# Output stage of two scan layers: scaling moved from GpSimd to ScalarE, and the code of a position arranged as a pipeline

## The chip, the cores and the metric

The kernel runs on one core of one Trainium2 chip. The metric is the device time of one execution in microseconds (us). Times of several executions are given as a median with the lowest and the highest. The profile is that of one further execution, and its span is the time from its first to its last instruction. Engine names are those of the profile: PE is TensorE, PEld its weight loads, DVE is VectorE, ACT is ScalarE, POOL is GpSimd, and SP is the engine that issues most DMAs.

## The reference

The input `x` has 4 batches of 64 x 64 positions with 192 channels, in float32. Two layers follow each other, and each adds its result to its input:

```python
x = x + _L0_conv_ref(_gn(x), ...)
x = x + _L1_conv_ref(_gn(x), ...)
```

Both layers have the same frame. The input is normalised by groups and projected to 768 channels, of which 384 are the values and 384 the gate `z`. The values go through four selective scans (by rows, by columns, and both backwards; layer 1 of the reference has a small convolution in front), and the four results are summed to `y`, with 384 channels at each of 4096 positions. What the change touches is what comes after that sum, here as the second layer has it:

```python
y = y1 + y2 + y3 + y4
mu = jnp.mean(y, axis=-1, keepdims=True)
var = jnp.mean(jnp.square(y - mu), axis=-1, keepdims=True)
y = (y - mu) * jax.lax.rsqrt(var + 1e-05) * gamma + beta
y = y.reshape(B, H, W, D_INNER) * jax.nn.silu(z)
return y @ W_out
```

So each position is normalised over its own 384 channels, scaled and shifted by channel, multiplied by the gate, and projected back to 192 channels.

## The kernel before

Layer 1 below is the reference's layer 0, layer 2 its layer 1. `FirstLayer.run` is called once for each of the 4 batches: it projects, scans (most of the time), and calls `finish` with a list of this one batch. `SecondLayer.run` is called once for all batches: it projects, prepares and scans the four, then calls the same `finish` with a list of four. So `finish` runs five times in an execution: four times with one batch, once with four. In the profile the tiles of layer 1 carry `_f` at the end of weight names, those of layer 2 `_s`; results of layer 1 go to `mid`, those of layer 2 to `out`.

`finish` works on tiles of 512 positions (`LC`), 8 of them in a batch (`NCH`), called positions 0 to 7 in this text. One tile holds `yt`, the summed `y` with positions on the 128 partitions (4 blocks, `NJ`, of 384 channels), and `zg`, the gate with channels on the partitions (3 blocks, `ND`, of 512 positions). Its steps are:

- `start` (L865) is called once for a batch. It issues the loads of `yt` and `zg` of all 8 positions (L870, L873) and the Silu of each `zg` on ScalarE (L874). Then, in two groups, positions 0 and 1 and positions 2 to 7, it takes mean and variance of every position on VectorE (L882, L883, into `mv`), the square root on ScalarE (L885) and the reciprocal on VectorE (L886, `rs`), and lets GpSimd subtract the mean and multiply by `rs`, in place, one block of 128 positions with 384 channels in an instruction (L891): four instructions for a position.
- The loop at L897 then goes through the positions: TensorE turns the 12 squares of 128 x 128 into `vp` with channels on the partitions (L905), ScalarE copies each of the three `vp` to `v` with scale gamma and bias beta (L908), VectorE multiplies `v` by the gate (L911), TensorE multiplies by `w_out` into four `op` (L916), VectorE adds the layer's input `xl` to each (L919), and SP stores the result (L920).
- For layer 2, `start` of the next batch stands in the code after position 4 of the current one (L921).

The order of the instructions on each engine in `finish` isn't written by hand. The scans are enclosed in a manual schedule, but `finish` is not: a scheduler orders what is there by the code order, the data dependences and the free buffers of the pools. Each engine then takes its instructions strictly in that order, SP its DMAs too. The pools that matter are `fy` and `fz` with 10 buffers each (so `yt` and `zg` of 8 positions and of 2 more), `fw` with 3 (`v`, `ot`, `st`), `fl` with 3 (`xl`), `fm` with 4 PSUM banks (`vp`) and `fo` with 4 (`op`).

In the built program before, TensorE's order in layer 1 is: transposes of positions 0 and 1, products of 0 and 1, transposes of 2 to 4, products of 2 to 4, transposes of 5 to 7, products of 5 to 7.

Of the kernel before, what the change touches and what calls it, by code (L numbers as in the profile page):

```python
# [10 lines left out]
F32 = mybir.dt.float32  # L11
AF = mybir.ActivationFunctionType
ALU = mybir.AluOpType

NB, HW, CH = 4, 64, 192
L = HW * HW
DI, NS, DR, KD = 384, 16, 12, 4
ND = DI // 128
CB, NC2 = 96, 2
LC = 512  # L20
NCH = L // LC
# [3 lines left out]
NJ = LC // 128  # L25
# [377 lines left out]
class FirstLayer:  # L403
# [449 lines left out]
    def finish(self, batches):  # L853

        nc, tc = self.tc.nc, self.tc
        with ExitStack() as ctx:
            pool = lambda name, bufs, **k: ctx.enter_context(tc.tile_pool(name=name, bufs=bufs, **k))
            py, pz, pl, ps, pw = pool("fy", 10), pool("fz", 10), pool("fl", 3), pool("fs", 2), pool("fw", 3)
            pm = pool("fm", 4, space=bass.MemoryType.PSUM)
            po = pool("fo", 4, space=bass.MemoryType.PSUM)  # L860
            w_out = ctx.enter_context(tc.tile_pool(name="fc", bufs=1)).tile([128, ND, CH], F32, name="w_out")
            nc.sync.dma_start(w_out, self.w["w_out"])
            pos = lambda a, t: a[t * LC : (t + 1) * LC, :].rearrange("(j p) c -> p j c", p=128)

            def start(y, gate):  # L865

                yts, zgs = [], []
                for t in range(NCH):
                    yt = py.tile([128, NJ, DI], F32, name="yt")
                    nc.sync.dma_start(yt, pos(y, t))  # L870
                    yts.append(yt)
                    zg = pz.tile([128, ND, LC], F32, name="zg")
                    nc.sync.dma_start(zg, gate[t])  # L873
                    nc.scalar.activation(zg, zg, AF.Silu)  # L874
                    zgs.append(zg)
                for lo, hi in ((0, 2), (2, NCH)):
                    n = (hi - lo) * NJ
                    mv = ps.tile([128, n, 2], F32, name=f"mv{lo}")
                    for t in range(lo, hi):
                        st = pw.tile([128, NJ, nc.vector.BN_STATS_DIM], F32, name="st")  # L880
                        for j in range(NJ):
                            nc.vector.bn_stats(st[:, j, :], yts[t][:, j, :])  # L882
                            nc.vector.bn_aggr(mv[:, (t - lo) * NJ + j, :], st[:, j, :])  # L883
                    rs = ps.tile([128, n], F32, name=f"rs{lo}")
                    nc.scalar.activation(rs, mv[:, :, 1], AF.Sqrt, bias=self.ln_eps)  # L885
                    nc.vector.reciprocal(rs, rs)  # L886
                    for t in range(lo, hi):
                        for j in range(NJ):
                            i = (t - lo) * NJ + j
                            part = yts[t][:, j, :]  # L890
                            nc.gpsimd.tensor_scalar(part, part, mv[:, i, 0:1], rs[:, i : i + 1], ALU.subtract, ALU.mult)  # L891
                return yts, zgs

            ready = start(batches[0][2], batches[0][3])
            for b, (src, dst, _, _) in enumerate(batches):
                yts, zgs = ready
                for t in range(NCH):  # L897
                    yt, zg = yts[t], zgs[t]
                    xl = pl.tile([128, NJ, CH], F32, name="xl")
                    nc.sync.dma_start(xl, pos(src, t))  # L900
                    v = pw.tile([128, ND, LC], F32, name="v")
                    for d in range(ND):
                        vp = pm.tile([128, LC], F32, name="vp")
                        for j in range(NJ):
                            nc.tensor.transpose(  # L905
                                vp[:, j * 128 : (j + 1) * 128], yt[:, j, d * 128 : (d + 1) * 128], self.ident
                            )
                        nc.scalar.activation(  # L908
                            v[:, d, :], vp, AF.Identity, bias=self.beta[:, d : d + 1], scale=self.gamma[:, d : d + 1]
                        )  # L910
                    nc.vector.tensor_mul(v, v, zg)  # L911
                    ot = pw.tile([128, NJ, CH], F32, name="ot")
                    for j in range(NJ):
                        op = po.tile([128, CH], F32, name="op")
                        for d in range(ND):
                            nc.tensor.matmul(  # L916
                                op, v[:, d, j * 128 : (j + 1) * 128], w_out[:, d, :], start=(d == 0), stop=(d == ND - 1)
                            )
                        nc.vector.tensor_add(ot[:, j, :], op, xl[:, j, :])  # L919
                    nc.sync.dma_start(pos(dst, t), ot)  # L920
                    if t == NCH // 2 and b + 1 < len(batches):  # L921
                        ready = start(batches[b + 1][2], batches[b + 1][3])


class Chunk:
# [651 lines left out]
```

## Time and profile before

| what | before |
|---|---|
| median of 3 runs | 11391.58 us (11390.1 to 11404.04) |
| span of the profiled execution | 11398.9 us |
| busy: PE, DVE, ACT, POOL | 84%, 85%, 85%, 79% of the span |
| mean granted TensorE clock | 0.926 of full speed |
| one output stage of layer 1, first `yt` load to last add | 2401.3 to 2501.8 us, the other three alike |
| output stage of layer 2 | 11095.2 to 11392.4 us |

A group of the profile names the line, the engine, the operation with its output and inputs, the shapes and the count; then come its total busy time, the mean of one, and the idle time of its engine just before it with what ended that idle time. A float32 matmul leaves two records, so the 768 products of L916 stand there as 1536. The view by windows gives the busy time of every engine in a stretch, the clock that TensorE was granted (1.00 is full speed), the share in which the 16 DMA engines were busy, and what they moved. The chain of waits follows the end back to what released it. An average over the whole execution says little here, since the scans take over four fifths of it and load all engines evenly; the output stages have to be read by themselves.

### The profile page before, as it was taken

The numbers are of one execution on the slowest core, as the hardware profiler recorded it, in microseconds if no ns is written. First come the engines' busy times: TensorE is split into PE (matmuls) and PEld (weight loads), VectorE is DVE, ScalarE is ACT, GpSimd is POOL, SyncE is SP. The second block draws the span as 40 slices with busy tenths as digits, with TensorE's granted clock in tenths as the row PEclk, the third lists the DMA queues.
The fourth block names the chain that finished last, engine by engine and source line by source line (L and its number), as shares of the span: only waits on it lengthen the run. The fifth ranks groups of instructions, "written<-read, shape, count | busy, mean of one in ns | idle before, by whom it ended". The sixth has DMA issues, their size and how long they took to land. (4 is left out here: it accounts for less than half of the span.)

```text
span 11398.9 us, 171795 instructions
## 1 busy us (share of the span) xinstructions
PE 9629.2 (84%) x61449; PEld 7328.0 (64%) x61449; DVE 9660.8 (85%) x11508; ACT 9638.7 (85%) x16730; POOL 9049.1 (79%) x3032
## 2 busy tenths in 40 slices
PE   7998888878998888878988888779988888788667
PEld 4776666655776666646766666647766666555356
DVE  4999899966999899948999899849998999788455
ACT  5999999957999999939999999849999999665554
POOL 3999899956999899938999899839998999700468
PEclk8999999988999999988999999979999999889678
DMA  4333334444333334443333334433333443433446
GB/s 125 108 105 97 94 99 98 100 127 122 108 103 100 93 99 99 97 156 97 109 102 96 96 97 103 123 119 108 108 99 94 98 103 98 128 120 127 144 117 238
DMA packets 831027, 1269.85 MB, mean 111 GB/s; under 512 B 99002, under 2 KB 514631, under 8 KB 829652
## 3 DMA queue, kind: packets, MB, share of 16 engines
q1 hardware_dynamic: 825300, 1252.49, 39.3%
q0 software_dynamic: 4864, 6.29, 0.4%
q8 instruction: 488, 8.00, 0.3%
q14 instruction: 375, 3.07, 0.1%
HBM read 958.19 MB, written 300.42 MB: 110 GB/s over the span
## 5 line engine op out<-in xcount | busy, mean ns | idle before, releaser
L738 POOL TENSOR_TENSOR h<-h,bct 128x1536 f32<-128x1536 f32 x2048 | 7062.7, 3470 | 577.6 <-DVE carry L734 475.8
L724 DVE TENSOR_TENSOR_SCAN h<-a,carry,x 128x512 f32<-128x512 f32 x5376 | 6605.9, 1267 | 226.8 <-PE x L716 184.5
L716 PE MATMUL x<-ident,xT 128*128 128x128 f32 x24576 | 4000.0, 287 | 815.7 <-DVE h L724 713.6
L699 ACT ACTIVATE xT<-dtuT,bT 128x384 f32<-128x384 f32 x8192 | 4360.0, 610 | 91.6 <-PE x L716 87.0
L716 PEld LDWEIGHTS x<-ident,xT 128*128 128x128 f32 x24576 | 2803.7, 145 | 2139.0 <-DVE h L724 926.3
L711 ACT ACTIVATE a<-dt,A_log_f 128x512 f32<-128x512 f32 x6144 | 3978.8, 717 | 0.0
L751 PE MATMUL yp<-ident,h 128*128 128x128 f32 x24576 | 3703.4, 277 | 9.3 <-POOL h L738 9.1
L751 PEld LDWEIGHTS yp<-ident,h 128*128 128x128 f32 x24576 | 2945.6, 144 | 78.8 <-issue 63.1
L615 PE MATMUL dp<-xd,w_dtb_f 13*128 13x512 f32 x1536 | 890.1, 663 | 208.0 <-DVE dt L644 206.9
L724 DVE TENSOR_TENSOR_SCAN h<-a,x 128x512 f32<-128x512 f32 x768 | 899.0, 1207 | 191.2 <-PE x L716 113.4
L628 POOL TENSOR_SCALAR wl<-e 128x1536 f32<-128x1536 f32 x128 | 189.3, 1479 | 699.0 <-ACT e L624 381.0
L891 POOL TENSOR_SCALAR yt<-yt,mv,rs 128x384 f32<-128x384 f32 x256 | 466.9, 1837 | 200.1 <-DVE rs L886 187.0
L490 PE MATMUL pp<-xT,w_in 96*128 96x512 f32 x1152 | 536.9, 617 | 0.0
L615 PEld LDWEIGHTS dp<-xd,w_dtb_f 13*128 13x128 f32 x1536 | 238.7, 192 | 452.1 <-DVE dt L644 336.1
L745 PE MATMUL yp<-yold,ident 128*128 128x512 f32 x768 | 440.8, 659 | 72.6 <-DMA yold<-y 72.6
L621 ACT ACTIVATE e<-dp 128x512 f32<-128x512 f32 x384 | 224.8, 585 | 307.8 <-DVE dt L644 153.5
L1094 DVE SCALAR_TENSOR_TENSOR acc<-pad,conv_w_s,acc 128x2048 f32<-128x2048 f32 x192 | 439.2, 2343 | 52.6 <-ACT acc L1092 51.9
L641 POOL TENSOR_TENSOR e<-e,wl 128x1536 f32<-128x1536 f32 x128 | 444.9, 3476 | 0.3
L638 POOL TENSOR_TENSOR e<-e,dt 128x1536 f32<-128x1536 f32 x128 | 442.8, 3459 | 0.3
L905 PE MATMUL vp<-ident,yt 128*128 128x128 f32 x768 | 163.6, 361 | 305.4 <-POOL yt L891 303.6
L1075 POOL MEMSET pad<- 128x66 f32 x12 | 1.9, 159 | 508.1 <-DVE acc L1094 489.3
L490 PEld LDWEIGHTS pp<-xT,w_in 96*128 96x128 f32 x1152 | 222.4, 198 | 253.4 <-issue 244.6
(171 smaller groups left out, 7173.9 us busy)
## 6 DMA issues: line engine op xcount, KB each, us to landing
bct<-xp SPq DMA_DIRECT2D x1024, 512.0 KB, 4.9
uT<-uT SPq DMA_DIRECT2D x64, 768.0 KB, 4.7
yold<-y SPq DMA_DIRECT2D x64, 768.0 KB, 8.0
y<-yt SPq DMA_DIRECT2D x64, 768.0 KB, 4.3
uT<-uT SPq DMA_DIRECT2D x128, 384.0 KB, 5.3
yold<-y SPq DMA_DIRECT2D x128, 384.0 KB, 5.3
y<-yt SPq DMA_DIRECT2D x128, 384.0 KB, 4.6
yt<-y SPq DMA_DIRECT2D x64, 768.0 KB, 10.4
```

Source lines behind the costliest of these rows:

```text
L490: self.tc.nc.tensor.matmul(pp, self.w_in[:, i, e * 128 : (e + 1) * 128], self.xT[:, i, t * LC : (t + 1) * LC], start=(i == 0), stop=(i == ...
L615: nc.tensor.matmul(self.dp[d], w, self.xd[0 : DR + 1, :], start=True, stop=True)
L638: nc.gpsimd.tensor_tensor(self.e, self.e, self.dt, ALU.subtract)
L641: nc.gpsimd.tensor_tensor(self.e, self.e, self.wl, ALU.add)
L699: nc.scalar.mul(xTs[g][:, j, :], it.dtuT[:, j * DI : (j + 1) * DI], it.bT[:, j, n : n + 1])
L711: nc.scalar.activation(as_[g][:, d, :], it.dt[:, d, :], AF.Exp, scale=scale)
L716: nc.tensor.transpose(xs[g, d][:, j * 128 : (j + 1) * 128], xTs[g][:, j, d * 128 : (d + 1) * 128], ident)
L724: nc.vector.tensor_tensor_scan(along(hs[g][:, d, :], it.k), along(as_[g][:, d, :], it.k), along(xs.pop((g, d)), it.k), 0.0 if it.first els ...
L738: nc.gpsimd.tensor_tensor(hs[g], hs[g], bc(cs[g - n % 2][:, n % 2, :], 1, ND), ALU.mult)
L745: nc.tensor.matmul(it.yp[b], ident, yo, start=True, stop=False, skip_group_check=True)
L751: nc.tensor.matmul(it.yp[b][:, i * 128 : (i + 1) * 128], hs[g][:, d, j * 128 : (j + 1) * 128], ident, start=False, stop=n == NS - 1, is_tr ...
L891: nc.gpsimd.tensor_scalar(part, part, mv[:, i, 0:1], rs[:, i : i + 1], ALU.subtract, ALU.mult)
```

## The change

`start` no longer scales the positions. It computes one more small vector per group, `off`, which is minus the mean times `rs`, on VectorE, and hands out `rs` and `off` for each position. A new function `gated` does, for one position, the scaling in place on ScalarE (`yt * rs + off`, four instructions), then the transposes, the copies to `v` and the product with the gate. A new function `out` does the load of `xl`, the products with `w_out`, the adds and the store. The loop runs over all positions of all batches in one list: `gated` of position t + 1 stands ahead of `out` of position t, also from one batch to the next, and `start` of the next batch stands at position 4 as before, though now ahead of that position's `out`. Nothing is left for GpSimd in `finish`. The pools keep their sizes.

```diff
             def start(y, gate):
-                yts, zgs = [], []
+                r = []
                 for t in range(NCH):
...
                     rs = ps.tile([128, n], F32, name=f"rs{lo}")
                     nc.scalar.activation(rs, mv[:, :, 1], AF.Sqrt, bias=self.ln_eps)
                     nc.vector.reciprocal(rs, rs)
+                    off = ps.tile([128, n], F32, name=f"off{lo}")
+                    nc.vector.scalar_tensor_tensor(off, mv[:, :, 0], -1.0, rs, ALU.mult, ALU.mult)
                     for t in range(lo, hi):
-                        for j in range(NJ):
-                            i = (t - lo) * NJ + j
-                            part = yts[t][:, j, :]
-                            nc.gpsimd.tensor_scalar(part, part, mv[:, i, 0:1], rs[:, i : i + 1], ALU.subtract, ALU.mult)
-                return yts, zgs
+                        part = slice((t - lo) * NJ, (t - lo + 1) * NJ)
+                        r[t] += [rs[:, part], off[:, part]]
+                return r
+
+            def gated(yt, zg, rs, off):
+                for j in range(NJ):
+                    part = yt[:, j, :]
+                    nc.scalar.activation(part, part, AF.Identity, scale=rs[:, j : j + 1], bias=off[:, j : j + 1])
+                v = pw.tile([128, ND, LC], F32, name="v")
+                for d in range(ND):
+                    vp = pm.tile([128, LC], F32, name="vp")
+                    for j in range(NJ):
+                        nc.tensor.transpose(
+                            vp[:, j * 128 : (j + 1) * 128], yt[:, j, d * 128 : (d + 1) * 128], self.ident
+                        )
+                    nc.scalar.activation(
+                        v[:, d, :], vp, AF.Identity, bias=self.beta[:, d : d + 1], scale=self.gamma[:, d : d + 1]
+                    )
+                nc.vector.tensor_mul(v, v, zg)
+                return v
+
+            def out(src, dst, t, v):
+                xl = pl.tile([128, NJ, CH], F32, name="xl")
+                nc.sync.dma_start(xl, pos(src, t))
+                ot = pw.tile([128, NJ, CH], F32, name="ot")
+                for j in range(NJ):
+                    op = po.tile([128, CH], F32, name="op")
...
+                    nc.vector.tensor_add(ot[:, j, :], op, xl[:, j, :])
+                nc.sync.dma_start(pos(dst, t), ot)
-            ready = start(batches[0][2], batches[0][3])
-            for b, (src, dst, _, _) in enumerate(batches):
-                yts, zgs = ready
-                for t in range(NCH):
...
-                    if t == NCH // 2 and b + 1 < len(batches):
-                        ready = start(batches[b + 1][2], batches[b + 1][3])
+            flat = [(b, t) for b in range(len(batches)) for t in range(NCH)]
+            ready = {0: start(*batches[0][2:])}
+            v = gated(*ready[0][0])
+            for i, (b, t) in enumerate(flat):
+                if t == NCH // 2 and b + 1 < len(batches):
+                    ready[b + 1] = start(*batches[b + 1][2:])
+                more = None
+                if i + 1 < len(flat):
+                    b1, t1 = flat[i + 1]
+                    more = gated(*ready[b1][t1])
+                out(batches[b][0], batches[b][1], t, v)
+                v = more
```

In the built program after, TensorE's order in layer 1 is: transposes of positions 0 and 1, products of 0 and 1, transposes of 2 and 3, products of 2, then transposes of t + 1 and products of t in turn up to 7. In layer 2 it is the same within a batch; from one batch to the next, the products of the last three positions stand behind the first transposes of the new batch.

More of the change, by code (lines that the diff above doesn't have):

```diff
@@ L870, in start @@
                     nc.sync.dma_start(yt, pos(y, t))
-                    yts.append(yt)
                     zg = pz.tile([128, ND, LC], F32, name="zg")
@@ L874, in start @@
                     nc.scalar.activation(zg, zg, AF.Silu)
-                    zgs.append(zg)
+                    r.append([yt, zg])
                 for lo, hi in ((0, 2), (2, NCH)):
@@ L881, in start @@
                         for j in range(NJ):
-                            nc.vector.bn_stats(st[:, j, :], yts[t][:, j, :])
+                            nc.vector.bn_stats(st[:, j, :], r[t][0][:, j, :])
                             nc.vector.bn_aggr(mv[:, (t - lo) * NJ + j, :], st[:, j, :])
@@ L892, in start @@
-                return yts, zgs
-            ready = start(batches[0][2], batches[0][3])
-            for b, (src, dst, _, _) in enumerate(batches):
-                yts, zgs = ready
-                for t in range(NCH):
[L898 to L901, printed above, removed]
-                    for d in range(ND):
[L903 to L909, printed above, removed]
-                        )
[L911 to L920, printed above, removed]
-                    if t == NCH // 2 and b + 1 < len(batches):
-                        ready = start(batches[b + 1][2], batches[b + 1][3])
@@ new lines, in out @@
+            def out(src, dst, t, v):
[4 more added lines that the diff above has]
+                    op = po.tile([128, CH], F32, name="op")
+                    for d in range(ND):
+                        nc.tensor.matmul(
+                            op, v[:, d, j * 128 : (j + 1) * 128], w_out[:, d, :], start=(d == 0), stop=(d == ND - 1)
+                        )
+                    nc.vector.tensor_add(ot[:, j, :], op, xl[:, j, :])
+                nc.sync.dma_start(pos(dst, t), ot)
```

## The prediction

> **What bounds the kernel now.** I read the page's groups first, because the diff touches one function, the output stage `finish`: which instruction there is long, and who waits for it.
>
> ```profile
> L891 POOL TENSOR_SCALAR yt<-yt,mv,rs 128x384 f32<-128x384 f32 x256 | 466.9, 1837 | 200.1 <-DVE rs L886 187.0
> L905 PE MATMUL vp<-ident,yt 128*128 128x128 f32 x768 | 163.6, 361 | 305.4 <-POOL yt L891 303.6
> ```
>
> GpSimd scales the positions (466.9 us), and TensorE stood idle 303.6 us for it. The scans' work cannot hide that, since each output stage runs after its scans. Next the busy time of each engine by stage: layer 2's output stage, then one output stage of layer 1 in tens of microseconds.
>
> ```profile
> 11095.00:11392.50 297.50, 208.15 (x1153) 191.14 (x1153) 167.75 (x425) 137.57 (x153) 238.27 (x128) 0.80 0.73 249
> 2401.30:2501.90 100.60, 56.39 (x289) 50.06 (x289) 43.47 (x106) 36.12 (x39) 56.76 (x32) 0.69 0.55 190
> ...
> 2421.00:2431.00 10.00, 5.77 (x22) 4.75 (x22) 2.57 (x3) 5.97 (x8) 6.19 (x4) 0.50 1.04 395
> 2451.00:2461.00 10.00, 5.28 (x21) 3.86 (x20) 1.76 (x1) 4.02 (x6) 10.00 (x6) 0.50 0.00 0
> 2471.00:2481.00 10.00, 10.00 (x64) 9.98 (x64) 5.49 (x12) 0.00 (x0) 10.00 (x7) 1.00 0.53 154
> ```
>
> Columns: PE, PEld, DVE, ACT and POOL busy, granted TensorE clock, DMA share, GB/s. In layer 2's stage GpSimd is busy 80%, TensorE 70%, and ScalarE, at 46%, is the emptiest. From 2451 GpSimd alone is full and TensorE runs at half clock; the loads (395 GB/s) are over by then. Then the timeline at the end of that stage:
>
> ```profile
> 2444.17 42.86 POOL L891 TENSOR_SCALAR yt<-yt,mv,rs 128x384 f32<-128x384 f32 x24 [16.98 <-DVE rs L886]
> ...
> 2480.74 3.26 PE L905 MATMUL vp<-ident,yt 128*128 128x128 f32 x26
> 2481.38 4.12 ACT L908 ACTIVATE v<-vp,beta_f,gamma_f 128x512 f32<-128x512 f32 x6 [11.86 <-PE vp L905]
> ...
> 2489.06 12.37 PE L916 MATMUL op<-w_out,v 128*128 128x192 f32 x72
> ...
> 2501.88 1.08 PE L454 MATMUL tp<-ident,xl 128*96 128x128 f32 x8 [0.45 <-DVE ot L919]
> ```
>
> The 24 pieces of positions 2 to 7 run at 1.79 us each; TensorE takes transposes of three positions and then the output products of three, so 12.37 us of products stand bare after the last piece; the next batch starts 0.05 us after the last add (2501.83). The other three batches repeat it (windows of 101, 101 and 102 us). For layer 2 the chain of waits shows the same pair:
>
> ```profile
> 11235.50 28.76 POOL yt L891 x15
> 11264.27 0.04 issue
> 11264.31 2.18 PE vp L905 x9
> 11266.49 16.97 PE op L916 x96
> ```
>
> **What the Trainium skill says.** (1) "ScalarE: Activation LUTs", section What ACT_TABLE_LOAD costs: an activation takes 186 ns, 93 more for each per-partition operand, 0.833 ns an element, and neighbours overlap by 93. The trace agrees: 512 columns with scale and bias as operands (L908) would be 798 and took 777; 384 with one (L699) would be 599 and took 610. (2) Same page, Table sets: identity is in every set, so a scaling between Silu and Sqrt needs no load. The trace agrees: at 11285.02 nine L908 run right behind the Sqrt at L885. (3) "TensorE: Matmul & The Clock Gate", Part 1: half clock until about 3.4 us of sustained work. The rows above show 0.50 beside gaps and 1.00 when full. (4) "GPSIMD Engine Reference", Engine selection: one-input work at roughly line rate. Here the measurement differs and decides: 384 columns with two per-partition operands took 1643 ns, 1536 with immediates (L628) 1477.
>
> **The change part by part.**
>
> Removed: 256 GpSimd pieces, 128 in each layer. Added: 256 ScalarE activations. From L908 less 128 columns (L711 717 less L699 610, so 107 ns) one is 670 ns alone; L908 in threes takes 2.11 us, a pitch of 0.667, so 0.56 in a row, 2.24 a position. Bounds 0.50 (L699's pitch) to 0.67. Further 16 small vector products `off` of 8 or 24 columns, priced as the reciprocals beside them (0.20 and 0.30 us); one per group lies on the path: 0.3 us a batch. No table load is added: the built program has as many as before. DMAs are the same in number. The program outside `finish` keeps its order but for one weight load and a handful of setup products between the layers, cost nothing: the long setup around them hides them.
>
> ScalarE then has per position Silu 1.40 (4 in 5.59), scaling 2.24 and three v 2.1: 5.7 us, where GpSimd had 4 x 1.64 = 6.6 alone and 4 x 1.86 = 7.4 in layer 2 (59.68 us for 32). The new activation waits for `off` from VectorE; behind it on ScalarE stand the v of the position before and the next Silu, and TensorE waits for both. VectorE per position: statistics 2.55, product 1.76, four adds 1.4, 5.7 us. TensorE at full clock: 12 transposes 1.5 (26 records in 3.26) and products 3.9 (an add every 0.975): 5.4 us; at half clock 2.6 (9 in 2.18) and 7.8. DMA: 2 x 768 KB and 2 x 384 KB, 2.36 MB, at the 393 GB/s of the full windows, 6.0 us. So GpSimd's 7.2 is followed by four engines within a tenth of each other. That is why I do not take the whole of the removed 467 us.
>
> Moved: in the built order TensorE has transposes of t+1 ahead of products of t for positions 2 to 6, one by one in place of by threes. The load of `xl` and the store of a position now follow the next position's work in the code; in the built SP queue three `xl` loads still stand ahead of the first `yt`, and the next batch's loads behind two stores, as before: nothing. GpSimd's queue has nothing left in the stage that could wait.
>
> *Layer 1, one batch.* On VectorE the statistics of positions 4 and 5 now stand ahead of the product of position 1. That product ends near 2431.1 (v ready at 2429.3, by laying ScalarE's order out with the times above; it was 2432.04). After it come 3 adds, statistics 6, 5 adds, statistics 7, some 7.7 us, then Sqrt 0.3, reciprocal 0.3, `off` 0.3: 2439.7 instead of 2444.1. ScalarE loads its table and does a last Silu (2.8): 2442.5. Six scalings (3.3), three v (2.1), the product (1.8): first output product at 2449.7. From there TensorE is the longest: 6 products x 3.9 and 4 transposes x 1.5, 29.4 us, and 1.7 for 3.4 us at half clock: 2480.8, with the last add 2481.2. ScalarE has 24 x 0.56 + 18 x 0.70 = 26 us from 2442.5, done at 2468.6 beside it; VectorE 19. Gain 2501.8 - 2481.2 = 20.6 us, for four batches 82. Ends: TensorE warm at once and ScalarE the limit, 27; TensorE cold for half of it, 12.
>
> *Layer 2.* The same start, 8693.9 us later by the first loads (2401.30 and 11095.21), gives `off` of the first batch at 11134 (GpSimd started 11139.06). ScalarE's work from there: 30 positions x 5.74, less 5 Silu done, plus 13 table loads x 1.28 and six Sqrt: 184 us. TensorE has 30 x 5.4 = 162, VectorE about 158, DMA 61.7 MB / 393 = 157. Between the batches the order is worse: products of positions 5 to 7 stand behind the first transposes of the next batch, and VectorE's adds behind its statistics. Laying the order out once, I get TensorE idle about 7 us and then 12 us of products in a row at each of three boundaries. I take a tenth of ScalarE's 184 as lost, 203, and 5 us for the last product and add: 11342 against 11392.4. Gain 51. Ends: no loss and no new waits, 68; a quarter lost, 25.
>
> Sum: 82 + 51 = 133 us. Against the profiled span of 11398.9 that is 11266. The profiled execution lies 7.3 us above the median of the three runs (11390.1 to 11404.04), so I forecast 11391.6 - 133 = 11258 us.
>
> **The rivals.**
>
> A. ScalarE is the only limit; TensorE stays warm. For: 10.00 of 10.00 busy at clock 1.00 from 2471. Against: 5.4 of 5.7 leaves nothing for gaps. 4 x 27 + 65 = 173 us: 11219.
>
> B. The loads become layer 2's limit. For: DMA shares of 1.02 to 1.05 in four of the stage's sixteen 20 us windows already, and 10 buffers, so the next batch's loads wait for a position to be used up and stand behind stores in SP's queue. Against: 75.5 MB need 192 us of 297. If each batch keeps 60 us in place of 63, layer 2 gives about 15: 82 + 15 = 97: 11295.
>
> C. Slower: TensorE stays at half clock. With transposes waiting 0.56 us on each scaling, its activity may never count as sustained. Then a position costs 2.6 + 7.8 = 10.4 us, more than GpSimd's 7.2; it decides once the mean clock falls below 5.4 / 7.2 = 0.75. Layer 1: first product 2449.7 + 6 x 7.8 + 4 x 2.6 = 2506.9, 5.5 us a batch lost, 22; layer 2: 32 x 10.4 = 333 against 297, 36. 11450. Against: an engine with that much work has no gaps, and full stretches show 1.00.
>
> D. The change doesn't do what it says: the scheduler still sets the order, and the products fall back into blocks of three at every position. The built order shows that only at batch boundaries; ScalarE would still replace GpSimd, some 70 us: 11322.
>
> **How the numbers follow.** Forecast 0.56, A 0.17, B 0.18, D 0.04, C 0.04, and 0.01 for no change. Own range of the forecast: layer 1 from 60 to 100, layer 2 from 35 to 62, so 95 to 162, 11230 to 11297. To leave out no more than 2 in 10 it takes in most of A and B: 11208 to 11308. About 0.2% (23 us) is what a measurement can tell here: faster 0.94 (forecast, A, B and D, less 0.01 for their tails), within 0.02, slower 0.04.
>
> **What would show it.** After: no GpSimd work in the five output stages; the scaling near 670 ns, 0.56 in a row; the last add of a layer 1 stage some 80 us after its first load, not 100; TensorE near full at clock 1.00 over the second half of it; layer 2's stage about 245 us with ScalarE near 85%. Wrong: half clock through these stages (C), VectorE or ScalarE waiting on loads for most of layer 2 (B), or a scaling near 1 us, which would make ScalarE the limit at 7.5 us a position and take the gain away.

## The result and the profile after

| what | before | after |
|---|---|---|
| median of the runs of one session | 11397.81 us (11390.1 to 11410.41, 4 runs) | 11279.01 us (11274.85 to 11280.24, 4 runs) |
| span of the profiled execution | 11398.9 us | 11278.4 us |
| the four output stages of layer 1, each | 95.9, 95.6, 95.6, 98.0 us | 74.0, 72.3, 73.5, 73.6 us |
| output stage of layer 2 | 292.4 us | 248.2 us |
| everything outside the five stages | 10721.4 us | 10736.9 us |

The ratio is 0.9894, with a 95% interval of 0.9877 to 0.9911: 118.8 us less in the medians, where 133 were forecast. A stage is counted here, and in every comparison below, from the start of its first statistics instruction (L881 after, L882 before) to the end of its last add (L920, L919). This leaves out the wait for the first load, which differs by a few microseconds from one layer to the other; counted from the first load, as in the prediction, layer 2's stage is some 5 us longer in both kernels (297.2 and 253.8).

The groups of the profile after that answer to the two shown of before. The columns are the same: busy time and mean of one, then idle time just before and what ended it.

```profile
L896 ACT ACTIVATE yt<-yt,off,rs 128x384 f32<-128x384 f32 x256 | 160.6, 702 | 0.0
L901 PE MATMUL vp<-ident,yt 128*128 128x128 f32 x768 | 138.2, 329 | 196.3 <-ACT yt L896 183.4 <-ACT v L904 11.8
```

The scaling now takes 702 ns on ScalarE where it took 1837 on GpSimd, and TensorE's idle time for it fell from 303.6 to 183.4 us. Of what is left, 151.5 us are the two long waits of each stage, for the loads and statistics of its first and its second group (21.8 to 29.3 and 6.4 us each).

The busy time of each engine by stretches: layer 2's stage, one of layer 1, and three tens of microseconds of that stage, which lie 3 us later than those shown of before because this batch's scans ended 3.3 us later.

```profile
11017.50:11271.50 254.00, 196.93 (x1153) 181.18 (x1153) 166.99 (x433) 211.71 (x281) 0.00 (x0) 0.83 0.85 292
2404.60:2483.40 78.80, 51.50 (x289) 46.92 (x290) 42.29 (x108) 54.37 (x71) 0.00 (x0) 0.74 0.69 239
2424.00:2434.00 10.00, 7.42 (x34) 6.29 (x33) 7.03 (x19) 9.35 (x12) 0.00 (x0) 0.63 1.05 399
2454.00:2464.00 10.00, 10.00 (x66) 9.96 (x65) 5.86 (x10) 9.14 (x16) 0.00 (x0) 0.93 0.29 80
2474.00:2484.00 10.00, 9.55 (x65) 9.26 (x63) 4.56 (x10) 2.11 (x3) 0.00 (x0) 1.00 0.81 247
```

GpSimd is at zero. In the stretch where GpSimd alone was full, and TensorE busy for 5.28 of 10 us at half clock, TensorE is now full at a clock of 0.93, and later at 1.00. In layer 2 ScalarE has become the busiest engine, 211.71 of 254, or 83%.

The timeline of the same stage of layer 1, from the second group's `off` to the next batch's first transposes:

```profile
2442.85 0.18 DVE L887 SCALAR_TENSOR_TENSOR off<-mv,rs 128x24 f32<-128x24 f32 x1
2445.19 3.68 ACT L896 ACTIVATE yt<-yt,off,rs 128x384 f32<-128x384 f32 x6
...
2452.85 5.30 PE L917 MATMUL op<-w_out,v 128*128 128x192 f32 x24
...
2459.30 4.07 PE L917 MATMUL op<-w_out,v 128*128 128x192 f32 x24
...
2463.20 1.47 PE L901 MATMUL vp<-ident,yt 128*128 128x128 f32 x12
...
2464.51 4.07 PE L917 MATMUL op<-w_out,v 128*128 128x192 f32 x24
...
2474.94 7.97 PE L917 MATMUL op<-w_out,v 128*128 128x192 f32 x48
```

One position's products follow the next position's transposes, every 5.21 us (2459.30 to 2464.51), without a gap. The bare 12.37 us of products of three positions at the end have become 3.9 us of one. TensorE sets this part now, as the prediction had it.

Layer 2 is less simple. Five stretches of 20 us of its stage:

```profile
11117.00:11137.00 20.00, 20.00 (x141) 19.92 (x140) 15.37 (x39) 19.94 (x28) 0.00 (x0) 1.00 1.01 352
11137.00:11157.00 20.00, 14.54 (x85) 12.33 (x84) 16.72 (x41) 19.55 (x28) 0.00 (x0) 0.80 1.00 359
...
11197.00:11217.00 20.00, 10.54 (x59) 7.64 (x57) 14.85 (x41) 18.07 (x24) 0.00 (x0) 0.75 1.03 377
11217.00:11237.00 20.00, 19.64 (x117) 19.60 (x118) 10.13 (x24) 19.49 (x31) 0.00 (x0) 0.91 0.57 163
11237.00:11257.00 20.00, 20.00 (x139) 19.91 (x138) 11.74 (x20) 9.61 (x15) 0.00 (x0) 1.00 0.54 158
```

Three things can be read here, and they point to three different limits. ScalarE is full nearly throughout. The DMA engines are nearly full too, until the loads end near 11217. And TensorE loses half of its time where a batch changes (10.54 of 20 at the third change), to be full afterwards and last to finish. The chain of waits passes through all three (products, copies to `v`, scaling, Silu, and the loads of gate and `y`), so it can't decide. The experiments have to.

### The profile page after: what moved, and what is told of

Same layout as the page of the kernel before. It is cut to its first block, busy times and chain, and to the rows that moved or that the text cites. A ratio compares the mean times of both kernels' runs of the same rounds, so it can differ in the third digit from the quotient of the medians.

```text
span 11278.4 us, 171696 instructions
## 1 busy us (share of the span) xinstructions
PE 9593.1 (85%) x61449; PEld 7301.6 (65%) x61449; DVE 9659.2 (86%) x11524; ACT 9787.2 (87%) x16986; POOL 8583.8 (76%) x2776
## 3 DMA queue, kind: packets, MB, share of 16 engines
q1 hardware_dynamic: 825300, 1252.49, 39.6%
## 5 line engine op out<-in xcount | busy, mean ns | idle before, releaser
L734 DVE TENSOR_REDUCE carry<-h 128x3 f32<-128x3 f32 x2048 | 322.7, 158 | 70.5
L644 DVE SCALAR_TENSOR_TENSOR dt<-dp,e 128x512 f32<-128x512 f32 x384 | 255.6, 666 | 74.6 <-POOL e L641 68.1
```

## The experiments

A table first, so that each can be found in it. The medians are of 4 to 12 runs. Beside these runs the kernel before had medians of 11397.81 to 11405.06 us, and each ratio is to the runs of before on the same chip. The kernel after was timed in one session alone, so a difference of up to some 7 us between its median and that of an experiment may be one of sessions. The stages are from one profile of each kernel. How far one profile can be trusted is seen in layer 1, whose stage is the same in the kernel after, e3_fewer_loads, e4_no_silu, e5_spread and e9_neither: its twenty values there lie between 71.8 and 75.0 us. So a few us in layer 2's stage, which is over three times as long, are not to be leaned on.

| kernel | median, us | ratio to before (95%) | layer 1, one stage (mean of 4) | layer 2 |
|---|---|---|---|---|
| before | 11397.81 | | 96.3 | 292.4 |
| after | 11279.01 | 0.9894 (0.9877 to 0.9911) | 73.3 | 248.2 |
| e1_order_alone | 11378.24 | 0.9978 (0.9969 to 0.9987) | 92.6 | 274.3 |
| e2_engine_alone | 11361.66 | 0.9965 (0.9952 to 0.9977) | 90.7 | 269.2 |
| e4_no_silu | 11270.93 | 0.9884 (0.9867 to 0.9900) | 73.9 | 244.0 |
| e5_spread | 11281.98 | 0.9895 (0.9878 to 0.9911) | 73.1 | 244.5 |
| e3_fewer_loads | 11270.19 | 0.9885 (0.9869 to 0.9902) | 73.1 | 234.9 |
| e9_neither | 11238.93 | 0.9859 (0.9843 to 0.9876) | 73.0 | 208.8 |
| e6_rows | 11300.46 | 0.9910 (0.9893 to 0.9926) | 77.6 | 254.6 |
| e11_gate_order | 11348.66 | 0.9947 (0.9930 to 0.9963) | 81.3 | 284.9 |
| e13_rows_pe | 11358.9 | 0.9963 (0.9951 to 0.9976) | 84.8 | 289.0 |
| e8_all | 11274.21 | 0.9889 (0.9872 to 0.9905) | 74.7 | 255.3 |
| e10_three_groups | 11252.67 | 0.9868 (0.9851 to 0.9884) | 69.3 | 244.6 |
| e12_both | 11336.24 | 0.9937 (0.9920 to 0.9954) | 79.1 | 288.1 |

### Which half of the change does it: the order or the engine

The order alone, from the kernel after:

```diff
-                        r[t] += [rs[:, part], off[:, part]]
+                        r[t] += [rs[:, part], mv[:, part, 0]]
...
-                    nc.scalar.activation(part, part, AF.Identity, scale=rs[:, j : j + 1], bias=off[:, j : j + 1])
+                    nc.gpsimd.tensor_scalar(part, part, mean[:, j : j + 1], rs[:, j : j + 1], ALU.subtract, ALU.mult)
```

> The new loop, with the scaling left on GpSimd (and no `off`). Theory of the prediction, that GpSimd's 6.6 to 7.4 us a position bound the stage: TensorE still follows GpSimd's pieces, and only the bare end gets shorter. In layer 1 the last piece ends near 2487, one position's transposes, v and products follow, last add near 2496 in place of 2501.8: 6 us a batch, 24 in four, and some 6 in layer 2, a sum of 30: 11368 us. Rival, that the blocks of three held the stage and the engine was a side matter: 80 us or more, 11318 or less.

The engine alone, from the kernel before:

```diff
+                    off = ps.tile([128, n], F32, name=f"off{lo}")
+                    nc.vector.scalar_tensor_tensor(off, mv[:, :, 0], -1.0, rs, ALU.mult, ALU.mult)
...
-                            nc.gpsimd.tensor_scalar(part, part, mv[:, i, 0:1], rs[:, i : i + 1], ALU.subtract, ALU.mult)
+                            nc.scalar.activation(part, part, AF.Identity, scale=rs[:, i : i + 1], bias=off[:, i : i + 1])
```

> The loop of before, with the scaling on ScalarE through `off`. If the engine is what mattered, this has the rest of the 119 us: 15 us of each batch in layer 1 and 30 in layer 2, 90 in all: 11308 us. (The prediction's rival D put the same case at 70: 11322.) If engine and order need each other, since ScalarE's scaling of later positions now stands ahead of the v of earlier ones in one queue, it has 40 or less: 11358 or more.

Measured: 24.6 us for the order (11402.85 to 11378.24), near the 30 expected. TensorE still waited 265.7 us for GpSimd's pieces, where it had waited 303.6:

```profile
L899 PE MATMUL vp<-ident,yt 128*128 128x128 f32 x768 | 160.1, 355 | 287.9 <-POOL yt L894 265.7 <-DMA zg<-gate 22.1
```

For the engine alone 41.2 us (to 11361.66), and not the 90 that I expected; this is what the rival said. Together they make 118.8, nearly twice the sum of the two. The timeline of e2_engine_alone in the first batch shows why. First ScalarE, then TensorE:

```profile
2442.86 14.45 ACT L893 ACTIVATE yt<-yt,off,rs 128x384 f32<-128x384 f32 x24
2457.22 4.76 ACT L910 ACTIVATE v<-vp,beta_f,gamma_f 128x512 f32<-128x512 f32 x7
```

```profile
2443.61 3.93 PE L907 MATMUL vp<-ident,yt 128*128 128x128 f32 x15 [6.38 <-ACT yt L893]
2447.80 0.33 PE L907 MATMUL vp<-ident,yt 128*128 128x128 f32 x1 [0.27 <-ACT yt L893]
2458.03 2.96 PE L907 MATMUL vp<-ident,yt 128*128 128x128 f32 x13 [9.90 <-ACT v L910]
```

In the code of before, the scaling of all six positions stands in `start`, ahead of the first `v`. On GpSimd that did little harm: the order alone is worth 3.6 us a batch there, since GpSimd has no other work in the stage. On ScalarE the 24 scalings stand in one row ahead of the copies to `v` in the same queue, the four `vp` buffers are full, and TensorE waits 9.90 us. So in layer 1 the faster engine only pays in full when the code also puts `v` of a position between the scalings of the later ones: the halves are worth 3.6 and 5.6 us a batch, and together 22.9. In layer 2, with 18.1 and 23.2 of 44.2, they nearly add up; why it is otherwise there was not looked into.

### What sets layer 2: ScalarE's work, the order at the batch boundaries, or the transfers

Less work for ScalarE, in layer 2 for batches 1 to 3 (`first` is false there):

```diff
-                    nc.scalar.activation(zg, zg, AF.Silu)
+                    if first:
+                        nc.scalar.activation(zg, zg, AF.Silu)
```

> The kernel after, but in layer 2 the gates of batches 1 to 3 are multiplied in without Silu: 24 activations of 1.49 us (36 us) and the table loads around them are left out of ScalarE's queue; loads and the order at the batch boundaries stay. Layer 2's stage takes 253.9 us now. If ScalarE's work sets it: 220 to 230 us, the whole 11245 to 11255. If the loads set it (rival B): 248 or more, 11273 or more. If what counts is TensorE's idle time at the three boundaries (some 16 us each beyond 5.2 us a position), which this leaves alone: between them, 238 to 246.

The same work in another order:

```diff
-                if t == NCH // 2 and b + 1 < len(batches):
-                    ready[b + 1] = start(*batches[b + 1][2:])
+                if t == 0 and b + 1 < len(batches):
+                    ready[b + 1] = []
+                    coming = steps(ready[b + 1], *batches[b + 1][2:])
+                for _ in range(2 if t == 1 else 1 if t < NCH - 1 else 0):
+                    if b + 1 < len(batches):
+                        next(coming)
```

`steps` does what `start` does, one position's loads, Silu and statistics at each call.

> The kernel after, but the next batch's loads, Silu and statistics are spread over the positions of the batch before it (one position of the next batch per position) in place of all eight in one place. Same instructions, same loads; layer 1 is unchanged. In the built order no three products are left behind the next batch's transposes. If the boundary order holds layer 2, TensorE keeps its 5.2 us a position until ScalarE's sum of some 187 us after the first batch's `off` (11057.8) becomes the limit: ScalarE ends near 11245, last add near 11254, 17 us less: stage 237, whole 11262. If loads or ScalarE alone already set the 254 us: within 4 us of it.

Neither did what the theory behind it asked for: layer 2's stage fell by 4.2 and by 3.7 us, hardly more than the spread. Counted from the first load e4_no_silu's took 249.7 us, which is where the rival with the loads had been put (248 or more). 36 us of work less on ScalarE, and the end hardly moved. The waits of e4_no_silu in layer 2's stage (total, times, longest) show where it was held instead, on TensorE and on VectorE:

```profile
PE op L918 <- DVE ot L921: 28.4, 3, 11.0
```

```profile
DVE st L882 <- DMA yt<-y: 39.6, 17, 17.2
```

At each of the three boundaries the products wait up to 11 us for VectorE's adds to free their PSUM buffers; the adds stand behind statistics in VectorE's queue, and the statistics behind loads of `y`. (Of the 39.6 us for these loads, the 17.2 lie at the start of the stage; at the three boundaries it is 4 to 5 us each, since VectorE has other work between the loads.) The products then start in blocks at 11102.94, 11159.56 and 11215.33, every 56.2 us, that is 7.0 us a position. In the kernel after they start at 11102.86, 11160.47 and 11217.36, every 57.3. And e5_spread, without the blocks, moves at the same 7.0 us a position (its products start at 11148.47, 11155.50 and 11162.53). Its stretches:

```profile
11110.00:11130.00 20.00, 15.95 (x104) 15.18 (x104) 13.63 (x36) 19.91 (x27) 0.00 (x0) 1.00 0.94 318
...
11150.00:11170.00 20.00, 17.15 (x117) 16.37 (x116) 16.37 (x41) 17.93 (x26) 0.00 (x0) 1.00 0.95 320
```

So I looked at the transfers again. The first two lines are the kernel after's transfers between 11077 and 11217, the third the busy times of a somewhat longer stretch:

```profile
DMA packets 32383, 45.94 MB, mean 328 GB/s; under 512 B 1221, under 2 KB 29765, under 8 KB 32374
q1 hardware_dynamic: 32374, 45.82, 94.7%
11057.00:11237.00 180.00, 147.20 (x853) 134.17 (x854) 123.77 (x322) 173.00 (x235) 0.00 (x0) 0.84 0.91 311
```

The DMA engines are busy 95% of the time and move 328 GB/s, not the 393 that I had reckoned with. The kernel after moves packets of 768 B (x and output), 1536 B (`y`) and 6144 B (gate), which took 41, 70 and 247 ns on average. A position has 512 of 768 B twice, 512 of 1536 B and 128 of 6144 B: (2 x 512 x 41 + 512 x 70 + 128 x 247) / 16 engines = 6.84 us. That is what the DMA engines need for a position if they never stop; the rate says the same (2.36 MB at 328 GB/s in 95% of the time are 6.83 us). ScalarE is as near its end: its 211.7 us of the stage are 6.6 us for each of 32 positions, and it was busy 96% from 11057 to 11237. My 6.0 us came from windows that hold loads of `y` and gate only.

To test it, 22 of 24 gate loads go, and ScalarE keeps its work:

```diff
+                for t in range(2):
+                    kept.append(pk.tile([128, ND, LC], F32, name=f"kept{t}"))
+                    nc.sync.dma_start(kept[t], batches[0][3][t])
...
-                    nc.sync.dma_start(zg, gate[t])
-                    nc.scalar.activation(zg, zg, AF.Silu)
+                    if first:
+                        nc.sync.dma_start(zg, gate[t])
+                    nc.scalar.activation(zg, zg if first else kept[t % 2], AF.Silu)
```

> The kernel after, but in layer 2 the gates of batches 1 to 3 aren't loaded: Silu reads one of two gate tiles kept from batch 0, so ScalarE's work is unchanged and 22 loads of 768 KB fewer run (two of the 24 are spent on the kept tiles). A position of these batches then needs 4.9 us of the DMA engines in place of 6.84. In the built order the products no longer fall into blocks of three (e5_spread had that alone, and was 3 us faster in the stage). If the transfers set layer 2: 15 to 20 us less, then ScalarE sets it, 11259 to 11264 in whole. If they don't: 5 us or less.

And both, no gate load and no Silu in these batches:

> Both at once: in layer 2 the gates of batches 1 to 3 are neither loaded nor put through Silu. e4_no_silu, with the loads kept, was 4 us faster in the stage, so ScalarE was not what held it. With the transfers at 4.9 us a position and ScalarE near 4.5, TensorE's 5.2 us should be what remains: from the first batch's first product of the second group (49 us after the first load) 30 positions of 5.2 us, 156, so a stage of some 205 to 215 us in place of 254, the whole 11230 to 11240. If something else holds layer 2 (the wait of VectorE's adds behind the statistics, the boundaries): 235 or more.

The stage fell by 13.3 us with fewer loads, a little short of the 15 to 20 expected, and by 39.4 with both (the median by 40.1, to 11238.93). Counted from the first load, e9_neither's stage is 214.3 us, inside the 205 to 215 expected. There TensorE is what is left: from 11060 on it is busy 18.5 to 20 us in each stretch of 20, as here:

```profile
11100.00:11120.00 20.00, 20.00 (x140) 19.85 (x139) 18.37 (x52) 18.55 (x30) 0.00 (x0) 1.00 0.89 288
```

The three limits can now be set side by side for layer 2's stage: with the transfers as they are, 244 us even with 36 us less for ScalarE (e4_no_silu); with ScalarE's work as it is and the transfers out of the way, 235 (e3_fewer_loads); with both out of the way, TensorE's 209. Taking away any one alone is worth 4 or 13 us, and taking away two is worth 39.

e3_fewer_loads and e9_neither change one thing more, since the scheduler no longer makes blocks of three there. Against e5_spread, which has no blocks either, e3_fewer_loads is 9.6 us shorter, so some 10 us of the 13.3 should be the loads; its order isn't the same, though. From e3_fewer_loads to e9_neither only the Silu goes in the code, and that is worth 26.1 us.

Two things stay open. No run leaves out the Silu and the blocks and keeps the loads; but in e4_no_silu the DMA engines were busy 94 to 100% in every 20 us from 11060 to 11220, so another order had little room there. And a gate load that is left out gives up its place in SP's queue as well as its traffic, which these runs don't separate.

### Larger packets, and the price of a stride

The transfers' cost lies partly in small packets, so the rows of a tile were arranged anew, four neighbouring rows to a partition, with larger packets for the same bytes. The rows' new order then has to meet the gate's order somewhere, and three runs put the stride on three engines. On VectorE:

```diff
-            pos = lambda a, t: a[t * LC : (t + 1) * LC, :].rearrange("(j p) c -> p j c", p=128)
+            pos = lambda a, t: a[t * LC : (t + 1) * LC, :].rearrange("(p j) c -> p j c", p=128)
...
-                nc.vector.tensor_mul(v, v, zg)
+                vr, zr = v.rearrange("c d (j p) -> c d j p", j=NJ), zg.rearrange("c d (p j) -> c d j p", j=NJ); nc.vector.tensor_mul(vr, vr, zr)
```

> The kernel after, but partition p of a tile holds the four neighbouring rows 4p to 4p+3 in place of rows p, p+128, p+256, p+384, in y, x and the output alike (the gate is read in the matching order by the product). Same bytes, same transfers, the same instructions in the same order on every engine; only the packets grow: y from 1536 to 6144 B, x and output from 768 to 3072 B. In the kernel after, packets of 768, 1536 and 6144 B took 41, 70 and 247 ns in layer 2, near 11 ns and 0.0384 ns a byte: a position's transfers fall from 6.84 to 6.02 us of all 16 DMA engines. If the transfers set layer 2's 7 us a position, its stage falls by some 15 us until ScalarE's sum (last add near 11254 on the scale of the kernel after) takes over, and `off` of each layer 1 batch comes some 3 us earlier: 12 + 15 = 27, whole 11252. If ScalarE or the order set it: 5 or less, 11274 or more. The gate read with a stride may cost VectorE something on its 1.76 us product.

On ScalarE:

```diff
-                    nc.scalar.activation(zg, zg, AF.Silu)
-                    r.append([yt, zg])
+                    zs = pg.tile([128, ND, NJ, 128], F32, name="zs")
+                    nc.scalar.activation(zs, zg.rearrange("c d (p j) -> c d j p", j=NJ), AF.Silu)
+                    r.append([yt, zs])
```

> e6_rows, but the stride is moved off VectorE: Silu reads the gate in the rows' order and writes a second tile in unit stride (gate tiles 4, the new ones 10), so the product is 1.75 us again and not 2.98. e6_rows lost 4 us in each layer 1 batch and 5 in layer 2 with VectorE at 6.9 us a position. If transfers set layer 2 and the strided product alone ate the gain: some 3 us a batch of layer 1 and 10 to 14 in layer 2, 11253 to 11257. If the stride costs ScalarE as much as VectorE (1.7 times, 1.0 us a position, 6.8 us in all): layer 2 gains nothing and layer 1 3 us a batch, 11268.

On TensorE:

```diff
-                            vp[:, j * 128 : (j + 1) * 128], yt[:, j, d * 128 : (d + 1) * 128], self.ident
+                            vp.rearrange("c (p j) -> c j p", j=NJ)[:, j, :], yt[:, j, d * 128 : (d + 1) * 128], self.ident
...
-                                op, v[:, d, j * 128 : (j + 1) * 128], w_out[:, d, :], start=(d == 0), stop=(d == ND - 1)
+                                op, v.rearrange("c d (p j) -> c d j p", j=NJ)[:, d, j, :], w_out[:, d, :], start=(d == 0), stop=(d == ND - 1)
```

> The rows of e6_rows (four neighbouring rows a partition, packets of 3072 and 6144 B, 6.02 in place of 6.84 us of transfers a position), with the stride left to TensorE: the transposes write PSUM with a stride of 16 B and the output products load their weights from v with one; gate, Silu and product are as in the kernel after, and so is the order of every engine's instructions. VectorE paid 1.23 us a position for such a stride (e6_rows), ScalarE 1.50 (e11_gate_order). If TensorE pays nothing: what larger packets alone are worth, some 3 us in each batch of layer 1 and 5 to 12 in layer 2 (ScalarE, whose sum ends near 10 us before the stage does, takes over), so 11255 to 11262. If TensorE's 24 weight loads a position get slower, by 0.1 us each, its 5.2 us a position become 7.6 and it sets both layers: 14 us a batch of layer 1 and some 30 in layer 2, 11360 or more.

All three lost against the kernel after: 21.5, 69.7 and 79.9 us. As a test of the transfers they failed, since what the packets gain can't be told from what the stride costs; only the prices can be read. One row from each profile's groups, in the order of the runs:

```profile
L907 DVE TENSOR_TENSOR v<-v,zg 128x1536 f32<-128x1536 f32 x64 | 191.5, 2992 | 41.6 <-ACT v L904 41.5
```

```profile
L875 ACT ACTIVATE zs<-zg 128x1536 f32<-128x1536 f32 x64 | 189.3, 2970 | 0.2
```

```profile
L917 PEld LDWEIGHTS op<-w_out,v 128*128 128x128 f32 x1536 | 370.6, 330 | 5.9 <-DVE ot L920 5.0 <-DVE v L907 0.9
```

With a stride of 16 B, VectorE's product takes 2992 ns in place of 1752, ScalarE's Silu 2970 in place of 1482, and TensorE's weight load 330 in place of 201.

The three are still useful as loads put on one engine each. Layer 2's stage grew by 6.4 us when VectorE got 1.24 us more a position (40 in all), by 36.7 when ScalarE got 1.49 more (48 in all), and by 40.8 when TensorE went from 5.21 to 6.96 us a position, all with fewer microseconds of transfers. So VectorE has room, and ScalarE has hardly any, which agrees with a ScalarE limit close under that of the transfers. (e11_gate_order also cuts the buffers of `zg` from 10 to 4, but its Silu waited for a gate load only once in layer 2's stage, for the first.) A run in which less work changes little (e4_no_silu) thus doesn't mean that more work would be free.

### A version that is faster than both

Three groups of statistics in place of two, on top of e5_spread:

```diff
-                for lo, hi in ((0, 2), (2, NCH)):
+                for lo, hi in ((0, 2), (2, 5), (5, NCH)):
```

> e5_spread with three groups of statistics (positions 0 and 1, 2 to 4, 5 to 7) in place of two, and the rows as in the kernel after. Aimed at what sets layer 1: TensorE's products of positions 2 to 7 all wait for the last load's statistics now (first product 48 us after the first load, then 5.2 us a position). With three groups, positions 2 to 4 are done while the last loads are read. Cost: one more Sqrt and two table loads, 2.9 us of ScalarE a batch. Layer 1's stage 70 in place of 78.3, 32 us in four; layer 2 as in e5_spread, 3 us less: 11244. If VectorE's or ScalarE's queue holds layer 1 (statistics of positions 5 to 7 behind the products of 2 to 4): 3 us a batch or less, 11265 or more.

11252.67 us, 0.9868 of before, where the kernel after has 0.9894: 26 us less than after in the medians, and its slowest run lies 18 us under the fastest of after. Layer 1's stage fell by 4.0 us to 69.3, half of the 8 expected, though the scaling of positions 2 to 4 now starts 12 us before the last group's `off`. Between the two groups' `off` (2428.7 and 2444.5) ScalarE also has three Silu and two table loads, so the products of these positions come out slower than TensorE could take them. In the profiles, four batches of layer 1 gave 16.2 us and layer 2 gave 3.5; what lies outside the stages differs by 13.5 more, with nothing changed there.

The same with the rows of e6_rows, and with those of e11_gate_order:

> A version meant to be faster: rows as in e6_rows, the next batch's start spread over the positions as in e5_spread, and three groups of statistics (positions 0 and 1, 2 to 4, 5 to 7) in place of two, so that layer 1's TensorE need not wait for all six loads: one Sqrt and two table loads (2.6 us of ScalarE) more a batch, for products of positions 2 to 4 (15.6 us of TensorE) that no longer come after the last load. In layer 1 some 10 us a batch from the groups and 3 from the rows, 52; in layer 2 some 15 to 20. The whole 11205 to 11215. If layer 1's stage is bound by something else after its last load: e6_rows' gain alone.

> e10_three_groups and e11_gate_order together: if both theories hold, the sum of their gains, 35 and 24, near 11220; if Silu's stride makes ScalarE the limit, e10_three_groups' time or more.

Neither held: 11274.21 and 11336.24 us, both above e10_three_groups. Both have the stride, on VectorE and on ScalarE.

## Why the prediction was right, and where its steps were not

The time fell inside the range and in the direction given. That alone says little of the mechanism: 11279 lies between the forecast's 11258 and rival B's 11295, somewhat nearer to B, and the forecast's errors partly cancel (layer 1 gained 9.7 us more than forecast, layer 2 some 7 less, and 15 were given back outside). Step by step:

- **The scaling.** Forecast 670 ns alone and 0.56 us in a row; measured 702 as the mean of all, and 0.60 in a row (24 in 14.45 us in e2_engine_alone). Inside the bounds of 0.50 to 0.67. GpSimd has no work left in the five stages.
- **Layer 1, start of the pipeline.** `off` of the second group was forecast at 2439.7 and the first product at 2449.7, on the times of before. With the 3.3 us by which this batch's scans ended later, 2443.0 and 2453.0; measured 2443.03 (2442.85 and 0.18) and 2452.85. So the two ends agree to 0.2 us, in part by luck: on the same shifted times, the product of position 1 ended 0.5 us later than laid out (2434.93) and what follows up to `off` was shorter by as much, and the six scalings began 0.6 us earlier (2445.19) and took 0.4 longer (3.68).
- **Layer 1, the rest.** Forecast 5.4 us a position, measured 5.21, with the last add at 2483.3 against 2484.5. TensorE's clock was 0.93 in the stretch in which the products begin and 1.00 at the end, and the first position's products took 5.30 us and not 3.9, so the slow start cost 1.4 us, where the forecast had 1.7. The gain was 91.7 us in four batches, not 82: the first batch gained 21.8 against the 20.6 forecast, and the other three, which I took as copies of the first, gained 23.3, 22.1 and 24.4.
- **Layer 2.** In the 207 us from `off` (11057.35) to its end at 11264.4 ScalarE worked 186 and stood idle 21; forecast 184 and a tenth lost. The stage then ended 7 us later; forecast 5. The gain was 44.2 against 51. The size was nearly right, and its reason was not, so that part of the agreement is luck. I put the loss down to the order at the boundaries, where products of three positions stand behind the next batch's transposes. e5_spread took that order away and got 3.7 us; and of ScalarE's 21 idle us only 7 lie before 11237, the other 13.6 in the last batch, where TensorE is full. The step that was wrong is the transfers' price, "2.36 MB, at the 393 GB/s of the full windows, 6.0 us": it measures 6.84, because x and output go in packets of 768 B. With that number the 61.7 MB of transfers are 179 us and not 157, beside ScalarE's 184: they stand level with it, and e4_no_silu, e3_fewer_loads and e9_neither agree with the two holding layer 2 together. It could have been seen in the profile of before, whose packets between 11140 and 11340 took 41, 70 and 254 ns.
- **The rivals.** A, a warm TensorE with ScalarE as the only limit, failed in layer 2. B had half of the mechanism, the loads, at the wrong size: layer 2 still gained 44, not 15. C failed: TensorE's clock was 0.93 to 1.00 where its products follow each other in layer 1, and 0.83 on average in layer 2's stage. D didn't come true, and e2_engine_alone shows what it would have cost: without the order, the engine is worth 41 us, where D was put at 70.
- **Outside the stages.** I counted nothing, and 15.4 us were given back there. Layer 1's and layer 2's gains add up to 135.9, the span fell by 120.5. In the twelve experiments the time outside the stages lies between 10716.9 and 10745.4 us, with a mean of 10733.9, and before's single profile has 10721.4. The first statistics of the first stage, ahead of which no edit stands in the program, start between 2398.1 and 2409.3 us in the fourteen profiles. Comparing the scans one by one, the two profiles drift apart in steps of 1 to 2 us in both directions, already in the first batch, which comes before anything that was changed. Whether there is a lasting cost of some 10 us in it, or only the spread of single executions (before's runs themselves reach from 11382.72 to 11417.75), these runs don't settle.

## What to carry to other kernels

Moving work to an idle engine and reordering the code can be worth little each and much together: when the new engine also feeds the next step, its queue has to alternate between the two, and here the code order made it do so. Before calling one engine the limit of a stage, work out every engine's and the transfers' time for one unit of work in that same mix. Limits that lie close together, here 6.84 us of transfers and 6.6 us of ScalarE a position, hide one another: removing one was worth 4 or 13 us and removing both 39, so a test needs both removed at once. Price the transfers by packets and not by the rate of the best window.

## What the hardware showed that I had not expected

Small packets cost more for a byte. Packets of 768, 1536 and 6144 B took 41, 70 and 247 ns on average, which fits 11 ns for a packet and 0.0384 ns a byte. The fit isn't exact: those of 3072 B in e6_rows took 140, and it gives 129. With 16 engines it is 300 GB/s for the smallest and 398 for the largest, and the share of busy time looks the same for both. The Trainium skill ("DMA: Bandwidth & Descriptors", Why small descriptors are slow) names a fixed overhead a packet and calls joining descriptors into one packet worthwhile only up to 256 B; here packets of 768 B moved a quarter less in the same time than those of 6144 B. No run here shows what larger packets alone would win.

A stride of 16 B between float32 elements in SBUF cost 1.7 times on VectorE, 2.0 on ScalarE and 1.6 on the weight load. The Trainium skill ("SBUF — State Buffer", Door 1: The DMA port swizzle) says that SBUF has lines of 16 B and that an access that crosses to a new line pays. That agrees, as each element of this stride lies in another line; but the page also gives 4 float32 as how far one can stride for free, and a stride of exactly 4 was not free here. The same place says that any non-contiguous access to PSUM slows matmuls down significantly. The transposes of e13_rows_pe, which write PSUM with a stride of 16 B, took 328 ns; without it, in the kernel after, they took 329. For these the measurement differs and decides.
